# Relational graph layer on one core: h of pairs three to five transposed by DMA, in place of quarter products for S1 T1

## The chip, the cores and the metric

One core of a Trainium2 chip runs the whole program. The metric is the device time of one execution in microseconds. Every time below was measured on the chip, and the profile is one execution as the hardware profiler took it. Engine names are those of the profile: PE is TensorE, PEld its weight loads, DVE is VectorE, ACT is ScalarE, POOL is GpSimd and SP is SyncE, which here only issues DMAs.

## The reference, cut to what matters

```
h = maximum(layernorm(x), 0)                      # x is [1250, 1024], float32
out = h @ root + bias
for r in range(8):                                # 20000 edges (src, dst), each with a type
    sums = segment_sum(h[src] * (edge_type == r)[:, None], dst, n)
    cnt  = segment_sum(edge_type == r, dst, n)
    out += (sums / maximum(cnt, 1)[:, None]) @ weight[r]
u = out
z = concatenate([u, h], 1) @ w_gate + b_gate
y = x + tanh(u) * z + h * (1 - z)
```

## The kernel before

The 1250 rows are ten blocks of 128 (the last has 98), taken in five pairs: pair i is blocks i and i + 5, numbered from 0, so pairs "three to five" of the title are i = 2, 3, 4. Eleven matrices (eight weights, root, two halves of the gate) are multiplied one after another; s counts the matrices. For s < 10 the operand is h, and it stays in SBUF transposed, in `h_op[i]`, seven slots of 128 x 4 x 128 float32: A11, A12, A22 and the Winograd sums S1, S2, S3 (in A21's place) and S4.

`product` (line 445) does one pair with one matrix as seven products of quarters instead of eight. One of them, `add` at line 461, is four matmuls of 128 x 512, which the trace shows as eight records. After each product PE's result leaves PSUM by a copy on ACT or an addition on DVE, and `done()` (line 464) makes a "call": `between(j)` lets other work be written into the instruction streams at that place. The engines' queues are in order, so the place of a call decides what waits behind what.

From the second matrix on, some of the seven products of two neighbouring pairs are themselves split into seven products of half size. Such a one is two matmuls of 128 x 256 (line 227). `First` (line 329) does it for A11, `Second` (line 194) for A12, `Third` (from s = 4 on) for S4, and `Fifth` (line 372, s = 1 to 4, `FIFTHS`) for S1 times T1. `Fifth` forms sums on DVE twice (lines 281 to 290), copies half-banks on ACT (lines 396, 404 and 411), adds on DVE (lines 406 and 417), and uses a PSUM bank for each of its two results, `ps_n` and `ps_m`. The rest of PSUM is a ring of three banks `ps` (line 123), two banks `ps_b`, in which a pair's main sum grows, and `ps_q`.

While the first matrix is multiplied (s = 0) two generators fill the calls. `norms` (line 1319) makes h for the pairs: statistics on DVE, the scaled relu on ACT (line 965), two stores of 512 KB to `h_dram` on SP (line 970), `transposed` (line 419: eight PE transposes per block into `ps` banks, copied out by ACT at line 433 and DVE at line 431), x + h on DVE, stored at line 976, and `left` (line 437) for the four sums on DVE. `index` (line 1380) sorts the edges into a table. In groups of four chunks of edges it makes one-hot matrices on ACT (lines 1154, 1156, 1215, 1216), counts and looks up with small matmuls on PE (lines 1168 and 1223), picks and ranks on DVE (lines 1208 to 1258), loads keys through SP (line 1187), and after every fourth group writes 16 columns of the table by indirect DMAs on POOL (line 1262). `zip_longest` (line 1389) moves both on by one step at each call, and `on` (line 1395) leaves out five places of each later matrix. The index ends during s = 3. Its rows are used from s = 5 on, when POOL gathers rows of the products (line 1437) and DVE adds them up (line 1442) beside PE.

Of the kernel before, what the change touches and what calls it, by code (L numbers as in the profile page):

```python
# [12 lines left out]
I16 = mybir.dt.int16  # L13
AF = mybir.ActivationFunctionType
# [6 lines left out]
def tile_rgcn_highway(  # L21
# [61 lines left out]
    TICK = 9  # L83
    FIFTHS = 4
# [38 lines left out]
    def bank():  # L123
        return psum.tile([P, 512], F32, name="ps", bufs=3)

    def sum_bank(odd):

        return psum.tile([P, CG, P], F32, name=("ps_n", "ps_m")[odd], bufs=1).rearrange(
            "p c k -> p (c k)")
# [137 lines left out]
    class Third:  # L267
# [24 lines left out]
        def hold(self):  # L292
            self.c0 = sum_bank(0)
            return self.c0
# [77 lines left out]
    class Fifth:  # L372

        def __init__(self, f, i, room, p5):
            b = f.place["t1"]
            self.b11, self.b12, self.b21, self.b22 = [
                b[:, k:k + 2, c:c + H] for k in (0, 2) for c in (0, H)]  # L380
            self.a11, self.a12, self.a21, self.a22 = [
                h_op[i + o][:, S1, k:k + 2] for o in (0, 1) for k in (0, 2)]
            self.t1, self.t2, self.s1, self.s2 = room
            self.p5 = p5

        def sums(self):
            Third.sums(self)

        def next_sums(self):
            Third.next_sums(self)  # L390

        def begin(self):
            self.to0 = sum_bank(0)
            self.x = bank()[:, :H]
            Second.add(self, self.x, self.a11, self.b11, True)
            nc.scalar.copy(self.to0[:, :H], self.x)

        def second(self):
            Second.add(self, self.to0[:, :H], self.a12, self.b21)

        def early(self):
            y = bank()[:, :H]
            Second.add(self, y, self.s1, self.t1, True)
            nc.scalar.copy(self.p5, y)
            Second.add(self, self.x, self.s2, self.t2)
            nc.vector.tensor_add(self.to0[:, H:], self.x, self.p5)

        def late(self):
            self.to1 = sum_bank(1)
            Second.add(self, self.x, self.s1, self.t1)  # L410
            nc.scalar.copy(self.to1.rearrange("p (a n) -> p a n", a=2),
                           self.x[:, None, :].to_broadcast([P, 2, H]))
            Second.add(self, self.to0[:, H:], self.s2, self.b22)
            Second.add(self, self.to1[:, :H], self.a22, self.t2)

        def fifth_to(self):
            nc.vector.tensor_add(self.to1[:, H:], self.to1[:, H:], self.p5)

# [17 lines left out]

    def left(aop, parts=range(4)):

        for k in parts:
            to, add, a, b = ((S1, True, A21, A22), (S2, False, S1, A11), (S4, False, A12, S2),  # L440
                             (S3, False, A11, A21))[k]
            (nc.vector.tensor_add if add else nc.vector.tensor_sub)(aop[:, to], aop[:, a],
                                                                     aop[:, b])

    def product(aop, w, to, between=lambda j: None, last=None, pieces=1, whole=True,
                fill=None, second=None, third=None, inner=None, first=None, early=None, own=(),
                aside=None, head=False, lone=False, odd=0, root=None):
# [21 lines left out]
        def filled(name):  # L469
            if fill and name in fill and fill[name]():  # L470
                done()
                return True
            return False
# [10 lines left out]
        def p7():  # L484
# [3 lines left out]
            if root and head:  # L488
                between(TICK)
                root.late()  # L490
                nc.scalar.copy(c22, c)
                root.fifth_to()
# [20 lines left out]
        def p1():  # L513
# [5 lines left out]
            if root and head:  # L519
                root.sums()  # L520
                first.fifth_to()
            nc.scalar.copy(c11, b)
            if root and head:
                root.second()
# [4 lines left out]
        def p5(c=None):  # L529
            if root:  # L530
                c = root.to1
            elif c is None:
                c = inner.hold() if inner and inner.holds else sum_bank(odd)
# [9 lines left out]
        if root and head:  # L543
            root.begin()
            c = root.to0
            if inner:
                inner.c0 = c
            b = p1()
        elif first and head and early is None and "first" not in fill:
            c = inner.hold() if inner else sum_bank(odd)  # L550
# [15 lines left out]
        if root and head:  # L566
            root.early()
            root.next_sums()
        if not filled("sixth") and root and head:
            done()  # L570
# [67 lines left out]
    def fifths(s):  # L638

        return 0 < s <= FIFTHS  # L640

    waiting, waiting_third, waiting_first, waiting_fifth = {}, {}, {}, {}
# [10 lines left out]
    def step(s, i, between=lambda j: None, second=None):  # L653
# [8 lines left out]
        if two and i % 2 == 0:  # L662
            waiting[i] = Second(fac[s], i), t[0]
            if fifths(s):
                waiting_fifth[s, i] = Fifth(fac[s], i, room, p5_room)
# [13 lines left out]
        def beside(j):  # L679
# [6 lines left out]
            if two and i % 2 == 0 and j == 3:  # L686
                if not root:
                    waiting_first[s, i].fifth_to()
# [14 lines left out]
            if (s, i, j) == (0, 0, 3) or (s > 0 and (i, j) == (3, int(thirds(s) or fifths(s)))):  # L703
# [28 lines left out]
        root = waiting_fifth.get((s, i - i % 2)) if two else None  # L732
# [11 lines left out]
        if two:  # L744
# [30 lines left out]
            elif i == 2 and root and q:  # L775
                fill = dict(seventh=lambda: (e.first(), q.second(q.c0), True),
# [1132 lines left out]
```

## Time and profile before

| what | value |
|---|---|
| median of three executions | 1391.94 us |
| range of the three | 1385.30 to 1395.03 us |
| the profiled execution | 1385.30 us |
| its span, first to last instruction | 1383.5 us |
| busy in that span: PE, DVE, POOL, ACT | 1335.2, 992.4, 575.9, 381.3 us |
| mean granted clock of PE | 0.986 |

The profile gives, for each engine, the time in which at least one of its instructions ran. A matmul's end is modelled, and consecutive matmuls overlap, so what one costs in a stream is read from start to start and not from its duration. In a timeline line, the first two numbers are start and length in us, `x8` is the number of records merged, and the square bracket gives how long the engine had been idle and who ended the wait. "remote" there means that the profile names no releaser.

### The profile page before, as it was taken

The page shows a single profiled execution, that of the slowest core. Times are in us where ns is not written, and L with a number is a line of the kernel's source. Part 1 is how long each engine was busy: PE and PEld are TensorE (multiplying, and loading weights), DVE is VectorE, ACT ScalarE, POOL GpSimd, SP SyncE. Part 2 cuts the span into 40 slices and gives each one's busy share as a digit, 9 for nine tenths or more (in the row PEclk, how much of TensorE's full clock was granted, in tenths as well). Part 3 has the DMA queues.
Part 4 walks back from the last instruction along what each step waited for, and adds up shares of the span by engine and source line. Part 5 has one row for each costly group of instructions (what it writes and reads, how often), then busy time and mean ns, then how long its engine had stood idle before and what let it go on. Part 6 is the DMA issues. An engine that isn't in the chain of part 4 may idle for free.

```text
span 1383.5 us, 13746 instructions
## 1 busy us (share of the span) xinstructions
PE 1335.2 (97%) x4264; PEld 746.0 (54%) x4264; DVE 992.4 (72%) x1905; ACT 381.3 (28%) x818; POOL 575.9 (42%) x509
## 2 busy tenths in 40 slices
PE   9999987889989999999999999999999999999997
PEld 5444544445645554665565565566556556544443
DVE  7765844476637575655888898798688789857875
ACT  3465534536441221221111112122111111221210
POOL 0005544435355224620345346554545556624631
PEclk9999989899999999999999999999999999999999
DMA  9766322524154326114556878987968976888971
GB/s 321 275 196 111 78 66 39 180 84 67 56 141 94 86 72 128 45 63 141 193 179 216 272 242 281 341 267 239 330 223 294 331 261 202 279 307 252 337 191 58
DMA packets 104322, 260.61 MB, mean 188 GB/s; under 512 B 20670, under 2 KB 32338, under 8 KB 104112
## 3 DMA queue, kind: packets, MB, share of 16 engines
q0 software_dynamic: 44064, 118.20, 27.0%
q1 hardware_dynamic: 44048, 109.48, 24.7%
q10 hardware_dynamic: 16128, 31.98, 8.1%
q8 instruction: 34, 0.56, 0.2%
q14 instruction: 48, 0.39, 0.1%
HBM read 202.34 MB, written 75.41 MB: 201 GB/s over the span
## 4 chain that ended last, share of the span: by engine, by line
PE 79%; issue 7%; DVE 3%; ACT 3%; POOL 3%; DMA 2%; another core or an unknown queue 2%; POOLq 0%; SPq 0%; ACTq 0%; DVEq 0%
PE ps_b L461 39%; PE ps L227 13%; PE ps_m L461 9%; PE ps_n L461 5%; PE ps_b L227 3%; PE ps_n L227 2%; PE ps_q L227 2%; PE ps_q L461 2%; DMA got<-y,idx 2%; PE ps L461 2%; PE ps_m L227 1%; POOL got L1437 1%; PE ps L426 1%; ACT is_lo L1154 1%
## 5 line engine op out<-in xcount | busy, mean ns | idle before, releaser
L461 PE MATMUL ps_b<-w,h_op 128*128 128x512 f32 x1464 | 667.0, 600 | 7.6 <-ACT row L564 6.8
L461 PEld LDWEIGHTS ps_b<-w,h_op 128*128 128x128 f32 x1464 | 277.0, 192 | 318.0 <-issue 300.8
L1437 POOL DMA_INDIRECT got<-y,idx x193 | 248.2, 1286 | 288.5 <-DVE u L1442 184.9
L1442 DVE SCALAR_TENSOR_TENSOR u<-got,w_of,u 128x1024 f32<-128x1024 f32 (+1 forms) x193 | 246.9, 1282 | 33.1 <-DMA got<-y,idx 29.2
L1262 POOL DMA_INDIRECT table<-row_col,at_i x157 | 170.5, 1086 | 204.8 <-DVE at_i L1258 127.3
L461 PE MATMUL ps_m<-w,h_op 128*128 128x512 f32 x352 | 158.8, 594 | 1.1 <-DVE row L324 1.1
L461 PEld LDWEIGHTS ps_m<-w,h_op 128*128 128x128 f32 x352 | 66.3, 190 | 77.2 <-issue 72.9
L461 PE MATMUL ps_n<-w,h_op 128*128 128x512 f32 x208 | 94.6, 593 | 0.0
L227 PE MATMUL ps<-inner,inner 128*128 128x256 f32 x360 | 92.3, 383 | 0.0
L227 PE MATMUL ps<-w,h_op 128*128 128x256 f32 x320 | 84.4, 387 | 3.3 <-ACT w L244 3.3
L564 ACT COPY row<-ps_b 128x512 f32<-128x512 f32 x54 | 31.6, 585 | 201.0 <-PE ps_b L461 186.7
L487 ACT COPY row<-ps_b 128x512 f32<-128x512 f32 x53 | 31.0, 585 | 197.4 <-PE ps_b L461 194.8
L227 PEld LDWEIGHTS ps<-inner,inner 128*128 128x128 f32 x360 | 68.6, 192 | 18.6 <-issue 9.9
L227 PEld LDWEIGHTS ps<-w,h_op 128*128 128x128 f32 x320 | 60.2, 192 | 30.5 <-issue 20.1
L227 PE MATMUL ps<-w,w 128*128 128x256 f32 x288 | 73.9, 393 | 2.7 <-ACT w L233 2.7
L608 ACT COPY row<-ps_b 128x512 f32<-128x512 f32 x40 | 23.4, 584 | 179.2 <-PE ps_b L461 131.0
L227 PEld LDWEIGHTS ps<-w,w 128*128 128x128 f32 x288 | 56.4, 197 | 23.3 <-issue 13.4
L493 DVE TENSOR_TENSOR row<-row 128x512 f32<-128x512 f32 x44 | 30.2, 687 | 47.9 <-ACT row L487 42.9
L461 PEld LDWEIGHTS ps_n<-w,h_op 128*128 128x128 f32 x208 | 39.2, 190 | 44.1 <-issue 43.1
L1244 DVE SCALAR_TENSOR_TENSOR junk<-k_bc,key_col,before 128x128 f32<-128x128 int16 x157 | 55.0, 350 | 4.2
L1231 DVE TENSOR_TENSOR own<-ps_q,is_at 128x160 f32<-128x160 f32 (+1 forms) x40 | 12.7, 318 | 58.3 <-remote 37.3
L1154 ACT ACTIVATE is_lo<-io,less_lo 128x128 bf16<-128x128 f32 x157 | 50.1, 392 | 8.2 <-remote 5.3
(248 smaller groups left out, 1634.1 us busy)
## 6 DMA issues: line engine op xcount, KB each, us to landing
y<-row SPq DMA_DIRECT2D x72, 512.0 KB
w<-in_L_gnn_weight_dram ACTq DMA_DIRECT2D x21, 1024.0 KB
w<-in_L_gnn_weight_dram SPq DMA_DIRECT2D x10, 1024.0 KB
w<-in_L_gnn_w_gate_dram ACTq DMA_DIRECT2D x6, 1024.0 KB
k_bc<-keys_dram SPq DMA_DIRECT2D x39, 128.0 KB
l_bc<-los_dram SPq DMA_DIRECT2D x39, 128.0 KB
h_dram<-h_op SPq DMA_DIRECT2D x9, 512.0 KB
u<-in_L_gnn_bias_dram SPq DMA_DIRECT2D x9, 512.0 KB
```

The lines of the kernel that those rows point to most:

```text
L227: nc.tensor.matmul(p, a[:, k, :], b[:, k, :], start=(fresh and k == 0), stop=(k == 1), skip_group_check=True)
L426: nc.tensor.transpose(p[:, i, :n], of[:n, k * P:(k + 1) * P], ident[:n, :n])
L461: nc.tensor.matmul(b[:, at], aop[:, i, k, :], w.of[i][:, k, at], start=(fresh and k == 0), stop=(k == KQ - 1), skip_group_check=True)
L487: nc.scalar.copy(d, b)
L493: nc.vector.tensor_add(c22, c if lone else c22, d)
L564: nc.scalar.copy(c12, b)
L608: nc.scalar.copy(c21, b)
L1154: nc.scalar.activation(is_lo[:, i, :], io, AF.Abs, bias=less_lo[:, c0 + i:c0 + i + 1])
L1244: nc.vector.scalar_tensor_tensor(junk, o["k_bc"][:, i, :], key_col[:, c:c + 1], before, op0=OP.is_equal, op1=OP.mult, accum_out=rank[:, c: ...
L1262: ins = nc.gpsimd.indirect_dma_start(out=table[:, :], out_offset=bass.IndirectOffsetOnAxis(ap=at_i[:n, c:c + 1], axis=0), in_=row_col[:n, ...
L1437: nc.gpsimd.indirect_dma_start(out=t[:n], out_offset=None, in_=y[g][:, :], in_offset=bass.IndirectOffsetOnAxis(ap=at[:n, d, k:k + 1], axis=0),
L1442: nc.vector.scalar_tensor_tensor(u[:n], t[:n], w, u[:n], op0=OP.mult, op1=OP.add)
```

## The change

Two parts are exchanged. `Fifth` and all that calls it are taken out: in the matrices s = 1 to 4, S1 times T1 is again one whole product for each pair. Its banks go: `ps` becomes a ring of four, the sum c of S1, S4 is held in a bank of that ring (in `ps_n` only where `Third` holds it, and for the last matrix), and `ps_m` is gone.

In the first matrix, h of pairs i = 2, 3, 4 no longer goes through PE. For each block ACT splits the float32 numbers into a plane of low and a plane of high two-byte halves (`in_halves`), a DMA issued by SP transposes the 128 x 2048 two-byte numbers from SBUF to SBUF (`turned`), and ACT and DVE write the halves back into place, one quarter each (`whole_again`). The work buffers are free slots of `h_op`, and `room_all`, which is the four former `inner` tiles as one. The steps of `norms` are put in a new order around this.

The two generators are joined anew: at calls that are marked HEAVY the index is not moved on. Four calls are marked, and one empty step more is in `columns`. In the later matrices `on` leaves out three places in place of five. Counted in the code, the first count step of the index comes one call later than before, from the fourth pair on each step comes four calls later, and the last step comes with matrix s = 4, first pair, call 2, where it came with s = 3, last pair, call 6.

```
-    FIFTHS = 4
...
-        return psum.tile([P, 512], F32, name="ps", bufs=3)
-
-    def sum_bank(odd):
-
-        return psum.tile([P, CG, P], F32, name=("ps_n", "ps_m")[odd], bufs=1).rearrange(
-            "p c k -> p (c k)")
+        return psum.tile([P, 512], F32, name="ps", bufs=4)
...
-    class Fifth:
...
+    def in_halves(of, n, to):
+
+        if n < P:
+            nc.gpsimd.memset(to[n // 32 * 32:], 0.0)
+        nc.scalar.copy(to.bitcast(U16)[:n].rearrange("p (h c) -> p h c", h=2),
+                       of.bitcast(U16)[:n].rearrange("p (c h) -> p h c", h=2))
+
+    def turned(of, to):
+
+        nc.sync.dma_start_transpose(to.bitcast(U16).rearrange("p (c r) -> p c r", r=P),
+                                    of.bitcast(U16))
+
+    def whole_again(aop, part, of, n):
+
+        of = of.bitcast(U16).rearrange("p (h a k r) -> p h a k r", h=2, a=2, r=P)
+        for a, to in enumerate(((A11, A12), (A21, A22))[part]):
+            (nc.vector.tensor_copy if a else nc.scalar.copy)(
+                aop[:, to].bitcast(U16).rearrange("p k (r h) -> p h k r", h=2)[..., :n],
+                of[:, :, a, :, :n])
+            if n < P:
+                nc.gpsimd.memset(aop[:, to, :, n:], 0.0)
...
         def p5(c=None):
-            if root:
-                c = root.to1
-            elif c is None:
-                c = inner.hold() if inner and inner.holds else sum_bank(odd)
+            if c is None:
+                c = inner.hold() if inner and inner.holds else held("ps_n")
                 add(c, S1, True)
...
-        if root and head:
-            root.begin()
-            c = root.to0
-            if inner:
-                inner.c0 = c
-            b = p1()
-        elif first and head and early is None and "first" not in fill:
-            c = inner.hold() if inner else sum_bank(odd)
+        if first and head and early is None and "first" not in fill:
+            c = inner.hold() if inner else bank()
             add(c, S1, True, ks=range(KQ // 2))
             b = p1()
             p5(c)
...
+        def turn(i, blocks, second, *of):
...
+            to, of = (room_all[:, :D], flat(second)), [flat(t) for t in of]
+            for part in range(2):
+                b = blocks[part]
+                in_halves(b.ht, b.n, of[part])
+                turned(of[part], to[part])
+                yield
+            for part in range(2):
+                whole_again(h_op[i], part, to[part], blocks[part].n)
+                yield
...
             both(*b2)
-            yield
+            for b in b1:
+                b.with_x()
+            yield
+            turn_of = turn(2, b2, h_op[3][:, 0:2], h_op[3][:, S2:S3 + 1], h_op[4][:, S2:S3 + 1])
+            next(turn_of)
             for b in b2:
                 b.store()
             yield
-            for b in b1:
-                b.with_x()
-            yield
-            factored(2, b2)
+            next(turn_of)
+            yield
             b2[0].with_x(b2[0].ht)
             b2[1].with_x()
+            x4 = [load_x(4, 0)]
+            yield
+            next(turn_of)
+            yield
+            next(turn_of)
+            yield
             left(h_op[2])
...
-        todo = (None for _ in zip_longest(norms(), index()))
+        def norms_and_index():
+
+            later = index()
+            for heavy in norms():
+                if not heavy:
+                    next(later)
+                yield
+            yield from later
+
+        todo = norms_and_index()
...
-                if s > 0 and (i, j) in ((0, 0), (1, 1), (1, 5), (3, 1), (NP - 1, 4)):
+                if s > 0 and (i, j) in ((0, 0), (1, 5), (NP - 1, 4)):
                     return
```

The lines of the diff that are not shown do the same for pairs i = 3 and 4, take the arguments and calls of `Fifth` out of `product`, `beside` and `step`, and add the type `U16`.

## The prediction

> **What bounds the kernel now.** I read the page's shares first, then the stretches, then TensorE's timeline, then who it waits for. Over the span PE is busy 1335.2 of 1383.5 us, so a step on PE's own list counts in full and one elsewhere only where PE waits for it. The page's mean hides three stages, which the stretches show (columns: us, then busy time and instructions of PE, PEld, DVE, ACT, POOL, then granted clock, DMA share, GB/s):
>
> ```profile
> core 0: us, PE busy (x) PEld busy (x) DVE busy (x) ACT busy (x) POOL busy (x), PEclk, DMA share, GB/s
> 50.00:100.00 50.00, 49.65 (x182) 24.97 (x181) 36.90 (x97) 31.78 (x69) 0.20 (x1) 1.00 0.64 228
> 200.00:250.00 50.00, 37.51 (x150) 23.17 (x149) 21.29 (x84) 22.45 (x57) 15.65 (x16) 0.88 0.20 37
> 400.00:500.00 100.00, 100.00 (x330) 57.62 (x330) 65.12 (x155) 23.46 (x51) 33.77 (x29) 1.00 0.41 105
> ```
>
> The first matrix (to about 126 us) fills PE; ACT has a third of the stretch free, DVE a quarter. The later matrices fill PE wholly. Between lies the index phase: PE idles and its clock falls. TensorE's timeline shows the places that the diff touches:
>
> ```profile
> 49.87 1.95 PE L426 MATMUL ps<-ident,h_op 128*128 128x128 f32 x16
> 51.65 3.60 PE L461 MATMUL ps_b<-w,h_op 128*128 128x512 f32 x8
> ...
> 65.39 1.47 PE L426 MATMUL ps<-ident,h_op 128*128 128x128 f32 x12
> 67.21 0.65 PE L426 MATMUL ps<-ident,h_op 128*128 128x128 f32 x4 [0.35 <-DVE h_op L431]
> 81.84 1.04 PE L426 MATMUL ps<-ident,h_op 128*128 128x128 f32 x8
> 93.62 0.84 PE L426 MATMUL ps<-ident,xt 98*128 98x98 f32 x8
> ```
> ```profile
> 159.56 1.03 PE L227 MATMUL ps<-inner,inner 128*128 128x256 f32 x4
> 160.42 1.03 PE L227 MATMUL ps_n<-w,inner 128*128 128x256 f32 x4
> 162.86 1.13 PE L227 MATMUL ps_m<-inner,h_op 128*128 128x256 f32 x4 [1.41 <-ACT ps_m L411]
> ...
> 247.01 0.39 PE L1223 MATMUL ps_q<-s_b,to_lo 128*128 128x40 bf16 x4 [10.17 <-DVE s_b L1208]
> 282.99 6.51 PE L461 MATMUL ps_b<-w,h_op 128*128 128x512 f32 x8 [4.68 <-ACT row L564]
> ```
>
> A row starts with start and duration; the bracket is the idle time before it and who ended it. Ends are modelled, so I take spacing from the next start: 51.65−49.87 = 1.78 us for 16 transposes; 160.42−159.56 = 0.86 for a quarter product (4 records); 3.43 for a whole product of 8.
>
> **The change part by part.**
>
> *Transposes off PE.* Pairs 2, 3 and 4 had the L426 rows at 49.87 (1.78 us), 65.39 to 67.70 (2.31 with its wait of 0.35), 81.84 (0.87 of spacing) and 93.62 (0.68): −5.6 us.
>
> *Seven quarters become two wholes.* `Fifth` gives 7 × 0.86 = 6.01 us for the S1·T1 of two pairs; two whole products take 2 × 3.43 = 6.87. That is +0.86 for each couple, two couples in each of the matrices 1 to 4: 8 × 0.86 = +6.9 us. DVE and ACT lose its sums (about 5.3 and 1.3 us a couple); in this stretch they are half idle, so I give nothing for that here, and a rival below prices it.
>
> *Fifth's own wait.* The row at 162.86 waits 1.41 us for ACT to empty ps_m. The trace has this wait four times (1.41, 1.41, 0.41, 0.41), and it goes with the products: −3.6 us. Late next is the ring, which follows.
>
> *Four ring banks in place of three and ps_m.* For matrices 1, 2 and 3, the first half of S1 of the first pair now takes the ring bank that the last pair's S4 has just filled, and so waits for the addition that empties it. In before that is the row on VectorE's timeline:
>
> ```profile
> 145.24 0.69 DVE L480 TENSOR_TENSOR row<-row,ps_m 128x512 f32<-128x512 f32 x1 [2.17 <-PE ps_m L461]
> ```
>
> S4's product ends at 145.20, the addition at 145.93: about 0.85 us with the hand-over, three times, +2.5 us. Queued behind it on PE is everything, as PE works in order. The upper end is that row falling behind a burst (rival 3).
>
> *ACT's splitting in the first matrix.* Each of six blocks gets a copy of 2048 two-byte elements and part of the joining; the evictions of L433 go. Nearest rows:
>
> ```profile
> 42.42 1.24 ACT L965 ACTIVATE h_op<-h_op,less,rs 128x1024 f32<-128x1024 f32 x1 [0.52 <-DVE less L949]
> ...
> 45.42 0.56 ACT L538 COPY row<-ps_m 128x512 f32<-128x512 f32 x1
> 50.51 0.60 ACT L433 ACTIVATE h_op<-ps 128x512 f32<-128x512 f32 x1 [4.04 <-PE ps L426]
> ```
>
> By the row of 1.24 for 1024 elements a split takes 2.5 us and a joined quarter 1.24, against an eviction of 0.60: 6 × (2.5 + 1.24 − 0.60) = +19 us on ACT between 42 and 112 us. ACT has some 18 free in each 50. What is queued behind a split are the copies of product banks (row 45.42), and PE waits for those only when one is late by more than a product of 3.43 us. I take +1 us. Ends: 0 if the splits fall between copies; 15 if each of six makes PE wait a whole split. DVE's joining adds some 3 us in a stretch with 13 free: nothing, and were that cover gone, 3 us.
>
> *The six transposing DMAs.* Each moves 512 KB from SBUF to SBUF on SP's queue; no row of before shows one. Call its time d. Low end: at the 415 GB/s that plain transfers reach in this stage, 1.3 us. High end: 2048 pieces of 256 bytes, each as costly as a mean packet of queue q1 (24.7% × 16 × 1383.5 / 44048 = 0.124 us), over 16 engines: 15.9 us. Small packets in this trace cost far less: q0 from 126 to 400 us has 3845 in 1.1% of 16 × 274 us, 12.5 ns each; twice that for the 256 bytes gives 24 ns and d = 3.1. I take 3, nearest to the small packets since the bytes are contiguous. SP's queue around them:
>
> ```profile
> 44.40 1.47 SPq L970 DMA_DIRECT2D h_dram<-h_op  x2
> 46.40 7.62 SPq L976 DMA_DIRECT2D xh_dram<-h_op  x3
> ```
>
> The xh stores of pair 1 (46.40) are issued ahead of them, the 1 MB of pair 2's h stores between the two. The first transpose can start near 48.5 (45.4 + 0.6 + 2.5); pair 2's S1 comes at 63.6 by now (67.82 less the transposes gone). With 2 us for joining and summing, nothing waits while d ≤ 3.8; pair 3 has room to 6.7, pair 4 to 5.6. The stall is 2(d−3.8) + 2(d−6.7) + (d−5.6), each term from its threshold: 0 at d = 3, 14 at d = 8, 53 at 15.9. I take 0.
>
> [...]
>
> *The index.* Counted in the code, its steps end four calls later than in before (about 10.5 us at 2.6 us a call), whatever the change says. Its readers have room: the index loads (POOL L836) end at 595.4 and the first DVE reader (L873) starts at 616.9, 21 us. Cost 0 while that cover lasts; were it gone, 10.5. The bursts of 16 indirect DMAs move with the steps and meet other products, priced below.
>
> *Sum:* −5.6 + 6.9 − 3.6 + 2.5 + 1 = +1.2 us. On the profiled execution (1385.3 us, span 1383.5) that is 1386.5. This execution is the lowest of the three, 6.6 below their median; on the median's scale it is 1391.9 + 1.2 = 1393.
>
> **The rivals.**
>
> *1. Transposes land late (slower).* For it: 2048 pieces each, on queues that already move up to 426 GB/s, behind stores. Against: room of 3.8 to 6.7 us. It decides at d = 8 (+14); at d = 9 the stall is 18.4, so 1393 + 18 = 1411.
>
> *2. The index phase heals (faster).* Between 126 and 420 us PE idles 34.5 us and spends 37.4 at half clock, some 14 us lost; nearly all lies in the table bursts of POOL L1262, where DVE and ACT get PE's results late:
>
> ```profile
> 246.40 0.33 DVE L1231 TENSOR_TENSOR own<-ps_q,is_at 128x160 f32<-128x160 f32 x1 [13.37 <-remote]
> ```
>
> For it: `Fifth` chains small products through DVE and ACT, and with it go 42 us of DVE and 10 of ACT, so PE meets fewer hand-overs in a burst. Against: the ten bursts stay, and 282.99 waits for a copy (L564) that stays too. It decides when over a quarter of the 48.5 us goes; a third is −16: 1393 − 16 = 1377.
>
> *3. The ring wait falls into the bursts (slower).* The new wait of 0.85 us needs DVE just after S4. In a burst a hand-over took 10.17 us (row 247.01). Three at 10 in place of 0.85 are +27 less some cover: 1393 + 25 = 1418. Against: a burst holds about 20 us in every eight calls, and S4 of the last pair at 145 fell outside. Two of three must be hit to pass 1%.
>
> *4. The index move does nothing.* Probably true, and inside the forecast.
>
> **How the numbers follow.** One per cent, about what a measurement here can tell from no change, is 14 us: faster is below 1378, slower above 1406. The forecast's case (costs as taken, bursts as costly as before) has 0.55, from 1384 to 1404 on its own: the 6.6 us between executions below, ACT's 10 above. Rival 1 gets 0.16, rival 2 0.15, rival 3 0.14. Faster 0.15 is rival 2; slower 0.30 is rivals 1 and 3; within 0.55. The range takes in rival 2's third and rival 3 with 3 us of scatter: 1377 to 1421; outside are d above 9.5 and a healing beyond a third.
>
> **What would show it.** No L426-like transposes on PE for pairs 2 to 4. The landing time of the transposing DMAs against 3 us, and whether PE's first products of pairs 2 to 4 name a joining step as releaser: if not, rival 1 falls. PE's idle time in 126 to 420 against 34.5 us, and its half-clock time against 37.4, decide rival 2. S1's first half after S4 three times with about 0.85 us of wait on DVE's addition; 5 or more is rival 3. S1 of whole products: 3.43 spacing. The prediction is wrong if PE waits in 40 to 126 us for more than 5 us in all, if the index phase moves by over 14 us either way, or if a wait stands before the first gather near 616 us.

## The result, and the profile after

| | time, us | against the kernel before |
|---|---|---|
| before, 20 runs | 1388.66 (1384.12 to 1396.63) | |
| after, 20 runs | 1381.85 (1374.99 to 1385.04) | ratio 0.9943, 95% interval 0.993 to 0.9957 |
| after once more, beside 13 runs of before (1390.92) | 1380.7 | ratio 0.9913, 0.9881 to 0.9945 |

The change made the kernel 0.6% faster, some 7 us, where 1 us slower was forecast. That is inside the 1% band and inside the range, but the sign is not the one that the sum gave, and the interval excludes it. The sum was near by luck: two of its terms, one wrong by 23 to 27 us and one by 16 to 22, cancel.

The two profiled executions (1385.30 and 1383.35 us) lie nearer to each other than the medians do. A second pair of profiles, taken in the experiments, is 5.6 us apart (spans 1385.2 and 1379.6), so I use both pairs. Three marks on TensorE's timeline divide an execution. They are the first half-size product of matrices 1, 2 and 3 (counted from 0), which has the same place in every version:

| us | matrix 1 begins | matrices 1 and 2 take | matrix 3 to the end of the span |
|---|---|---|---|
| before, two profiles | 133.90, 134.24 | 292.2, 291.7 | 957.4, 959.3 |
| after, two profiles | 128.17, 128.09 | 294.3, 293.0 | 959.1, 958.5 |

So the first matrix gains 5.7 to 6.2 us. The two matrices beside which the index runs lose 1 to 2 us, though whole products should cost them +3.4. What follows changes by less than two profiles of one kernel differ. Matrices 1 and 2 as one stretch, with the columns of the stretches shown before, first before, then after:

```profile
133.90:426.14 292.24, 257.74 (x951) 145.82 (x948) 167.48 (x609) 136.83 (x336) 135.36 (x127) 0.94 0.38 90
```
```profile
128.17:422.47 294.30, 262.00 (x913) 136.63 (x912) 152.75 (x587) 139.31 (x342) 139.19 (x131) 0.93 0.38 91
```

In both PE stands still for over 30 us and the granted clock is 0.93 to 0.94. Who ends the waits has changed. TensorE's timeline of after, the rows with a wait:

```profile
46.14 3.70 PE L430 MATMUL ps<-w,h_op 128*128 128x512 f32 x8 [0.35 <-ACT row L493]
...
175.93 1.13 PE L221 MATMUL ps<-w,w 128*128 128x256 f32 x4 [1.86 <-issue]
179.55 6.26 PE L430 MATMUL ps_b<-w,h_op 128*128 128x512 f32 x8 [2.49 <-ACT row L513]
210.89 0.26 PE L1154 MATMUL ps_q<-s_b,to_lo 128*128 128x40 bf16 x4 [3.77 <-issue]
216.20 6.71 PE L430 MATMUL ps_b<-w,h_op 128*128 128x512 f32 x8 [2.23 <-ACT row L513]
261.67 0.29 PE L1154 MATMUL ps_q<-s_b,to_lo 128*128 128x40 bf16 x4 [5.46 <-DVE s_b L1139]
...
328.94 6.65 PE L430 MATMUL ps_b<-w,h_op 128*128 128x512 f32 x8 [3.45 <-ACT row L513]
362.08 0.25 PE L1154 MATMUL ps_q<-s_b,to_lo 128*128 128x40 bf16 x4 [5.17 <-DVE s_b L1139]
410.16 5.31 PE L430 MATMUL ps_b<-w,h_op 128*128 128x512 f32 x8 [3.39 <-ACT row L481]
```

The 16 and 12 transposes on PE and the wait of 1.41 us for ps_m (row 162.86 of before) are gone. Every wait after 160 us stands in a run of sixteen table DMAs on POOL or ends at most 5.4 us behind it. With two more, they come to 32 us. In before such waits (4.11, 10.17, 4.68 and 1.93) come to 21, and others are mixed in. The row after a long wait is often stretched as well: the product at 179.55 takes 6.26 us, where one at full clock takes 3.60; from 178 to 184.5 us the granted clock is 0.50.

The new DMAs on SP's timeline, and two rows of ACT's:

```profile
48.61 3.72 SPq L393 DMA_TRANSPOSE inner<-h_op  x1
52.40 1.03 SPq L900 DMA_DIRECT2D h_dram<-h_op  x2
53.53 4.21 SPq L393 DMA_TRANSPOSE h_op<-h_op  x1
```
```profile
46.69 1.90 ACT L388 COPY h_op<-h_op 128x2048 uint16<-128x2048 uint16 x1 [0.60 <-ACT row L493]
...
59.50 1.34 ACT L400 COPY h_op<-h_op 128x1024 uint16<-128x1024 uint16 x1 [3.46 <-DMA h_op<-h_op]
```

The second transpose of the pair is issued from 53.53 on, and ACT, which waits for it, starts at 59.50. By their semaphores all six land 4.3 to 6.0 us after the start of the issue. SP needs 2.0 to 4.2 us to issue one, against 0.5 for a plain store of the same size (the row of two at 52.40; the 80 stores of L616, 72 of them of that size, have a median of 0.32 and at most 1.19, while a load of x at the start takes 2.52). Still PE waits only 0.35 us in the whole stretch from 40 to 126 us.

### The profile page after: what moved, and what is told of

Its sections match the earlier page's. It is cut to its first block, busy times and chain, and to the rows that moved or that the text cites. A ratio compares the mean times of both kernels' runs of the same rounds, so it can differ in the third digit from the quotient of the medians.

```text
span 1381.6 us, 13340 instructions
## 1 busy us (share of the span) xinstructions
PE 1337.4 (97%) x4120; PEld 723.2 (52%) x4120; DVE 957.3 (69%) x1825; ACT 386.7 (28%) x800; POOL 581.3 (42%) x510
## 4 chain that ended last, share of the span: by engine, by line
PE 83%; issue 4%; DMA 3%; another core or an unknown queue 3%; ACT 2%; DVE 2%; POOL 1%; SPq 1%; POOLq 0%; DVEq 0%
PE ps_b L430 40%; PE ps L430 16%; PE ps L221 13%; PE ps_n L430 4%; PE ps_b L221 3%; PE ps_q L221 2%; PE ps_q L430 2%; PE ps_n L221 1%; DMA xt<-in_x_dram 1%; DMA got<-hr_dram,node 1%; DMA w<-in_L_gnn_weight_dram 1%; ACT is_lo L1085 1%; POOL out_dram L770 1%; DMA k_bc<-keys_dram 1%
## 5 line engine op out<-in xcount | busy, mean ns | idle before, releaser
L1415 POOL DMA_INDIRECT got<-y,idx x193 | 251.1, 1301 | 286.9 <-DVE u L1420 179.1
L430 PE MATMUL ps<-w,h_op 128*128 128x512 f32 (+1 forms) x592 | 267.2, 593 | 0.3 <-ACT row L493 0.3
L430 PEld LDWEIGHTS ps<-w,h_op 128*128 128x128 f32 x592 | 112.0, 192 | 122.6 <-issue 117.1
L454 ACT COPY row<-ps_b 128x512 f32<-128x512 f32 x53 | 31.1, 586 | 194.5 <-PE ps_b L430 178.8
L430 PE MATMUL ps_n<-w,h_op 128*128 128x512 f32 x176 | 80.1, 592 | 0.0
L513 ACT COPY row<-ps_b 128x512 f32<-128x512 f32 x54 | 31.6, 586 | 163.1 <-PE ps_b L430 154.3
L221 PE MATMUL ps<-w,h_op 128*128 128x256 f32 x288 | 75.4, 385 | 0.0
L553 ACT COPY row<-ps_b 128x512 f32<-128x512 f32 x40 | 23.4, 585 | 170.1 <-PE ps_b L430 117.7
L221 PEld LDWEIGHTS ps<-w,h_op 128*128 128x128 f32 x288 | 54.6, 192 | 27.7 <-issue 22.1
L221 PE MATMUL ps<-inner 128*128 128x256 f32 x264 | 67.8, 379 | 0.0
L221 PEld LDWEIGHTS ps<-inner 128*128 128x128 f32 x264 | 50.1, 190 | 14.9 <-issue 8.4
L430 PEld LDWEIGHTS ps_n<-w,h_op 128*128 128x128 f32 x176 | 33.4, 190 | 39.5 <-issue 39.0
L481 ACT COPY row<-ps_b 128x512 f32<-128x512 f32 x54 | 31.7, 586 | 79.4 <-PE ps_b L430 67.0
```

Source lines behind the costliest of these rows:

```text
L221: nc.tensor.matmul(p, a[:, k, :], b[:, k, :], start=(fresh and k == 0), stop=(k == 1), skip_group_check=True)
L430: nc.tensor.matmul(b[:, at], aop[:, i, k, :], w.of[i][:, k, at], start=(fresh and k == 0), stop=(k == KQ - 1), skip_group_check=True)
L454: nc.scalar.copy(d, b)
L513: nc.scalar.copy(c12, b)
L553: nc.scalar.copy(c21, b)
L1415: nc.gpsimd.indirect_dma_start(out=t[:n], out_offset=None, in_=y[g][:, :], in_offset=bass.IndirectOffsetOnAxis(ap=at[:n, d, k:k + 1], axis=0),
```

## The experiments

All are named by what they differ in. Each group ran on a chip of its own, beside its own runs of the kernel before. In the third group that kernel took 1356 us and not 1389 to 1392, and this difference turned out to be part of the answer. The last column is from the one profiled execution of each kernel. For e1 and e3 that was the fastest of its kernel (5.6 and 6.9 us below the median), for e4 and e8 the slowest (4.8 and 4.7 above), so these four stretches are good to some 5 to 7 us.

| kernel | us | ratio to before, 95% interval | matrices 1 and 2, us |
|---|---|---|---|
| group 1: before | 1388.65 | | |
| e0_before_again | 1388.15 | 1.000, 0.9982 to 1.0018 | 291.7 |
| e1_no_fifth | 1364.98 | 0.985, 0.9821 to 0.9878 | 262.8 |
| e2_index_four_sooner | 1411.82 | 1.0178, 1.015 to 1.0207 | 298.2 |
| e3_transposes_on_pe | 1386.30 | 0.9985, 0.9967 to 1.0004 | 283.7 |
| group 2: before | 1391.73 | | |
| e4_no_fifth_index_later | 1388.97 | 0.9967, 0.9948 to 0.9987 | 294.5 |
| e5_no_fifth_fours | 1342.78 | 0.9649, 0.9603 to 0.9695 | 244.4 |
| e6_after_fours | 1345.28 | 0.9662, 0.9617 to 0.9708 | 252.4 |
| e7_after_twos | 1380.96 | 0.9925, 0.9903 to 0.9947 | 295.7 |
| group 3: before | 1356.26 | | |
| e8_after_fours_sooner | 1348.44 | 0.9947, 0.993 to 0.9963 | 249.3 |
| e9_after_eights | 1342.77 | 0.9904, 0.9887 to 0.992 | 244.7 |
| e10_before_fours | 1356.61 | 1.0005, 0.9989 to 1.0021 | 264.2 |
| e11_sooner_padding_on_dve | 1336.30 | 0.9858, 0.9842 to 0.9875 | 244.4 |
| group 4: before | 1390.92 | | |
| e12_after_again | 1380.70 | 0.9913, 0.9881 to 0.9945 | 293.0 |
| e13_no_fifth_again | 1370.51 | 0.9833, 0.98 to 0.9866 | 269.7 |
| e14_padding_on_dve_again | 1390.32 | 0.9983, 0.9954 to 1.0011 | 290.8 |
| e15_eights_again | 1373.15 | 0.9856, 0.9824 to 0.9887 | 276.5 |
| group 5: before | 1392.11 | | |
| e16_fours_padding_on_dve | 1341.07 | 0.9643, 0.9597 to 0.969 | 252.1 |
| e17_no_fifth_fours_again | 1342.90 | 0.9649, 0.9607 to 0.9691 | 244.3 |

### The change taken apart (group 1)

The control, the kernel before unchanged:

> The kernel before, once more, for a second profile of it and as a control of the comparison: ratio 1.000, within 0.002. If the index phase (126 to 420 us) varies from execution to execution, its loss on PE (time beyond the full-speed spacing of its products, 55.5 us in the first profile) comes out several us different here, and the longest waits stand at other places of the bursts; if it is fixed, the loss is 55 to 56 again.

The loss was the same, with the longest waits at the same runs (10.2 us near 247 and 4.1 near 198 again). Three others changed in size: 4.68 became 1.15, 1.19 became 2.89 and 1.30 became 3.17 us.

`Fifth` left out alone:

```
-    FIFTHS = 4
+    FIFTHS = 0
```

> The kernel before with S1 T1 of two pairs as two whole products in all matrices, nothing else of the change: transposes on TensorE, the index where it was (give or take a call). Theory A (products and their own waits only): 8 x 0.83 = +6.6 us of products, -3.6 of Fifth's waits, so +3 us, ratio 1.002. Rival B (the small dependent products also lengthen the table bursts, and that goes with them): 5 to 6 us less than A, ratio 0.998 or lower, and the index phase loses 45 to 50 us on PE in place of 52 to 55.

Measured: 24 us faster, far below what either theory allowed. The stretch of matrices 1 and 2 shows where:

```profile
134.18:397.00 262.82, 248.86 (x900) 132.13 (x896) 147.35 (x556) 132.51 (x323) 131.18 (x121) 0.98 0.49 100
```

It is 29 us shorter than in before, although it holds 3.4 us more of products. (This execution is 5.6 us below its median.)

The index moved on at every call, in the kernel after:

```
-        HEAVY = True
+        HEAVY = False
```

> The kernel after with the index moved on at every call, so that from the fourth pair on its steps come four calls sooner, as in the kernel before. Theory C (what the change gave beyond the transposes comes from where the table bursts fall among the products): 4 to 6 us slower than the kernel after, near 1387 us, ratio 0.998 to 1.000. Rival (placement does nothing in the mean): like the kernel after, 1382 us, ratio 0.994 to 0.996.

Both were wrong: 30 us slower than after. One wait makes 20 of them. TensorE's timeline, then POOL's, then VectorE's:

```profile
137.64 5.25 PE L430 MATMUL ps<-w,h_op 128*128 128x512 f32 x8 [20.07 <-issue]
...
191.34 0.25 PE L1154 MATMUL ps_q<-s_b,to_lo 128*128 128x40 bf16 x4 [4.60 <-DVE s_b L1139]
...
298.04 5.27 PE L430 MATMUL ps_b<-w,h_op 128*128 128x512 f32 x8 [4.62 <-ACT row L513]
```
```profile
115.79 1.16 POOL L1193 DMA_INDIRECT table<-row_col,at_i  x1 [14.61 <-DVE at_i L1189]
...
135.50 0.98 POOL L1193 DMA_INDIRECT table<-row_col,at_i  x1 [0.31 <-issue]
136.52 0.34 POOL L404 MEMSET h_op<- 128x120 f32 x2
```
```profile
136.89 2.74 DVE L411 TENSOR_TENSOR h_op<-h_op 128x512 f32<-128x512 f32 x4 [20.16 <-POOL h_op L404]
```

Two settings to zero of 0.2 us each (L404, the padding of the 98-row block) are queued on POOL behind sixteen indirect DMAs. DVE's sums wait for them, and PE for the sums. In after the same settings come before the first run, which the four HEAVY calls see to. The seven other waits of over 4 us in this kernel have one thing in common: PE goes on 2.4 to 2.9 us after the last table DMA of a run ended on POOL (at 188.9 and 295.2 us for the two shown).

The transposes of pairs 2 to 4 back on PE, in the kernel after:

```
-                in_halves(b.ht, b.n, of[part])
-                turned(of[part], to[part])
+                transposed(h_op[i], part, b.ht, b.n)
                 yield
...
-                whole_again(h_op[i], part, to[part], blocks[part].n)
```

> The kernel after with the transposes of pairs 2 to 4 back on TensorE, in the calls where the halves are split now; no splitting, no transposing DMAs, no joining. If the DMA transposes give what the removed products took: +5.7 us on the kernel after, 1387.5 us, ratio 0.999, all of it before 130 us. If they also cost something that no wait on PE shows (contention of the stores and weight loads behind them): less than +4, ratio under 0.998. If the index phase profits from the free DMA queues in another way, the difference is above 7.

Measured 1386.3, 4.4 above after. Matrix 1 begins at 134.38 in place of 128.17, so the 6.2 us before it are the transposes.

The three steps follow one another: before to e1_no_fifth 0.985, on to e3 0.9985, on to after 0.9943. Leaving `Fifth` out gives 24 us, something in the later index takes 19 back, and the transposes give 4 to 6.

### Where the index falls, and the runs of sixteen (group 2)

e1_no_fifth with four more empty steps in `columns`, so that all later index steps come four calls later:

```
             yield
             yield
+            yield
+            yield
+            yield
+            yield
```

> The kernel before without the seven quarter products (as e1_no_fifth, 1365 us), and every index step after the columns four calls later. Theory C (where the table bursts fall among the products decides, and four calls later is a bad place): the bursts cost PE 45 to 55 us in place of 24, 1385 to 1395 us. Rival D (the four ring banks, or the other places left out, made the kernel after slower than e1_no_fifth, not the four calls): 1365 us again, within 4.

Measured 1389.0, matrices 1 and 2 in 294.5 us. The four calls alone cost 16 us, most of what e3 had lost, so it is the place of the index and not the ring. PE's waits in matrices 1 and 2 grow with them from 14.0 us (e1) to 33.6.

Next, the table's indirect DMAs in groups of four, in e1_no_fifth and in after:

```
-    AT = 4
+    AT = 1
```

> As e1_no_fifth (1365 us), with the table's indirect DMAs issued four at a time, each group of four when its ranks are known, in place of sixteen at a time. Theory E (it is the unbroken run of sixteen that holds up the signals from PE): the index phase's loss falls from 24 to under 10 us, 1350 us. Rival F (each indirect DMA costs its share wherever it stands): 24 again, 1365 us; four DVE operations more per group stay off PE's path.

> As the kernel after (1382 us), with the table's indirect DMAs issued four at a time. Theory E: the loss of 55 us in the index phase falls under 15, 1342 us, and the kernel comes out 4 to 6 us ahead of e5_no_fifth_fours, which is what the transposes by DMA give. Rival F: 1382 us, within 5.

Both fell by more than 20 us. e6, expected 4 to 6 us ahead of e5, is 2.5 behind it: in matrices 1 and 2 the later place of the index still costs 8 us (252.4 against 244.4). Group 5 shows why. In e5 PE hardly waits in matrices 1 and 2:

```profile
138.36:382.74 244.38, 243.89 (x900) 130.21 (x897) 157.74 (x640) 132.95 (x323) 132.26 (x122) 1.00 0.53 107
```

The last of the group wrote the sixteen DMAs into the stream two at a call:

```
-                for c in range(c0, c1):
+                due.extend(range(c0, c1))
...
                     if f is None:
+                        scatter(2)
                         yield
```

> As the kernel after, with the same sixteen indirect DMAs made known together but issued two at a call over eight calls. Theory E: as e6_after_fours or 2 to 5 us better, near 1340 us; the waits on PE that end with a burst are gone. Rival F: 1382 us, within 5; then PE's waits are spread over the calls but sum up to 50 us.

Measured as after, but this tells nothing of theory E. POOL's timeline shows the same unbroken run:

```profile
155.96 1.18 POOL L1196 DMA_INDIRECT table<-row_col,at_i  x1 [8.04 <-DVE at_i L1189]
...
175.94 0.98 POOL L1196 DMA_INDIRECT table<-row_col,at_i  x1 [0.30 <-issue]
```

All sixteen wait for the same `at_i` and nothing else, and POOL takes one every 1.3 us, though they stand two at a call in the code. Groups of four are spaced because each needs ranks of its own.

### A chip without the hold-up, and the two causes apart (groups 3 and 4)

e8 has both edits, `AT = 1` and `HEAVY = False`, in the kernel after:

> The kernel after with the table's DMAs four at a time and the index moved on at every call (four calls sooner from the fourth pair on). Theory E (only long runs of these DMAs hurt; once they are gone the index's place is free): within 4 us of e6_after_fours, 1341 to 1349 us, where the same four calls cost 30 us with runs of sixteen. Rival: the place matters for another reason, and it is 10 us or more slower.

e9, the kernel after with groups of eight:

```
-    AT = 4
+    AT = 2
```

> The kernel after with the table's DMAs eight at a time, a dose between sixteen (55 us lost on PE between 100 and 450 us, 1382 us) and four (18 us, 1345 us). Theory E, a run holds a signal up until it ends: runs of 10 us, and part of them covered by work that PE already has: 25 to 40 us lost, 1352 to 1367 us. Rival (a threshold, such as more than eight of these DMAs in flight): as with four, 1345 us, within 3.

e10 is the kernel before with `AT = 1`:

> The kernel before, with its seven quarter products, and the table's DMAs four at a time. Theory E: what leaving the quarter products out saved (24 us) came from the runs of sixteen, so here they are worth what they were designed for: -6.6 of products, +3.6 of own waits against e5_no_fifth_fours, 1340 us, between 1336 and 1343. Rival B (the quarter products themselves cost the index phase, whatever the runs): 1355 to 1365 us.

e11 is e2 with one line more, in `whole_again`:

```
             if n < P:
-                nc.gpsimd.memset(aop[:, to, :, n:], 0.0)
+                nc.vector.memset(aop[:, to, :, n:], 0.0)
```

> As e2_index_four_sooner (1412 us), with the padding of the joined blocks set to zero on DVE in place of POOL. There the two settings stood behind sixteen table DMAs on POOL, and PE waited 20.2 us for the sums behind them. If that is the cause: 1412 - 20 = 1392 us, between 1386 and 1396, still above the kernel after by what the other runs of sixteen cost at that place. If PE's wait there is the same signal hold-up as elsewhere: 1407 us or more.

The kernel before took 1356 us on this chip, and fours left it there (1356.6), so times from this group do not compare with those of group 2. e8 and e9 tell little of theory E here; what they lose is mostly one wait each (6.58 and 7.29 us) for padding behind the table DMAs. e10 landed where rival B had put it. e11, with all its runs of sixteen, has no wait over 0.5 us in matrices 1 and 2. I therefore ran four kernels again, with what each would show on either kind of chip. The chip of group 4 was of the first kind:

> The kernel after, unchanged, beside the kernel before on one chip. In the last group of runs the kernel before took 1356 us where it had taken 1389 to 1392 on other chips, and no wait on PE ended with a run of sixteen table DMAs. Theory E with G (the signals are held up during those runs on some chips only; the quarter products' own waits are there on every chip): if before takes about 1356 here, after takes 1334 to 1342, some 18 us less; if before takes about 1390, after takes 1380 to 1384 again. Rival H (the gain is 7 us on every chip): near 1349 in the first case.

> The kernel before without the quarter products, unchanged from e1_no_fifth. Theory G (the quarter products bring waits of their own on PE and the clock's fall behind them, near 20 us net of their saving, wherever the runs of sixteen fall): 18 to 24 us less than before on this chip too, whichever its level. Rival (their removal only moved other work out of the runs of sixteen): with before at 1356, no gain or +3 us.

> The kernel after with the index sooner and the padding set to zero on DVE, unchanged from e11. With before at about 1390 (signals held up): 1412 less the 20 us behind POOL, 1388 to 1396. With before at about 1356: 1336 again.

> The kernel after with the table's DMAs eight at a time, unchanged from e9. With before at about 1390: theory E, between four at a time (1345) and sixteen (1382), 1352 to 1367 us; a threshold above eight: 1345. With before at about 1356: 1343 again, most of its loss being the one wait near 121 us.

e12, e13 and e14 came in as the theories with a hold-up said. e14 and e11 are one kernel on two chips, 1390 and 1336 us. A hand-over in a run of sixteen, in e14: VectorE's row, then the last DMA of the run on POOL, then TensorE's.

```profile
233.22 0.33 DVE L1162 TENSOR_TENSOR own<-ps_q,is_at 128x160 f32<-128x160 f32 x1 [10.76 <-remote]
```
```profile
229.75 0.98 POOL L1193 DMA_INDIRECT table<-row_col,at_i  x1 [0.31 <-issue]
```
```profile
223.20 0.26 PE L1154 MATMUL ps_q<-s_b,to_lo 128*128 128x40 bf16 x4
...
233.83 0.39 PE L1154 MATMUL ps_q<-s_b,to_lo 128*128 128x40 bf16 x4 [6.74 <-DVE s_b L1139]
```

PE made ps_q at 223.20, and DVE, idle since 222.46, reads it at 233.22, 2.5 us after the run ended (229.75 + 0.98). PE, which needs what DVE makes of it, waits 6.74 us. In e11, in the middle of a run (230.3 to 252.1), the same step on VectorE:

```profile
240.17 0.33 DVE L1162 TENSOR_TENSOR own<-ps_q,is_at 128x160 f32<-128x160 f32 x1 [4.25 <-PE ps_q L1099]
```

There PE's two groups of small products began at 239.77 and 239.88, so the hand-over took 0.3 us. So on the chips of groups 1, 2 and 4 PE's signals to DVE and ACT come late, by up to some 10 us, while a run of these DMAs goes on, and on that of group 3 they do not.

e15 missed its range (1373 against 1352 to 1367), and its rows say why. The first of TensorE's waits of over 2 us:

```profile
184.41 1.13 PE L221 MATMUL ps<-w,w 128*128 128x256 f32 x4 [2.67 <-issue]
189.02 5.98 PE L430 MATMUL ps_b<-w,h_op 128*128 128x512 f32 x8 [3.47 <-ACT row L513]
260.47 0.29 PE L1154 MATMUL ps_q<-s_b,to_lo 128*128 128x40 bf16 x4 [5.40 <-DVE s_b L1139]
```

By POOL's timeline two groups of eight stood together four times in this stretch, three times without a gap and once with one of 1.7 us (165.3 to 186.6 and 237.0 to 257.4 are the first two), and all waits of over 2 us lie in or just behind these four. The single eights, 10 us long (199.6 to 209.7, 219.8 to 229.8), have none. In e5 sixteen DMAs in fours, with gaps, take 24 us and cause no wait.

The second cause is seen in e10, on the chip without the hold-up. Its stretch of matrices 1 and 2, with the quarter products:

```profile
134.45:398.67 264.22, 249.28 (x952) 142.25 (x948) 179.34 (x697) 136.56 (x336) 135.00 (x126) 0.97 0.52 99
```

The whole products need 244.3 to 244.7 here, on either kind of chip (e5, e9, e11, e17), so the quarters should need 3.4 less, 241. They need 23 us more than that. Nearly two thirds of it stand as waits on TensorE's timeline:

```profile
163.34 1.13 PE L227 MATMUL ps_m<-inner,h_op 128*128 128x256 f32 x4 [1.42 <-ACT ps_m L411]
176.32 2.78 PE L227 MATMUL ps<-w,w 128*128 128x256 f32 x8 [2.65 <-ACT w L233]
...
233.83 3.70 PE L461 MATMUL ps_b<-w,h_op 128*128 128x512 f32 x8 [1.34 <-ACT row L522]
...
307.26 3.58 PE L227 MATMUL ps<-w,w 128*128 128x256 f32 x8 [2.65 <-ACT w L233]
```

With seven more, these come to 14.5 us; the granted clock of 0.97 in the row above, over 264 us, is another 8 or so. What stood before the second of them on ACT:

```profile
173.91 1.27 ACT L1154 ACTIVATE is_lo<-io,less_lo 128x128 bf16<-128x128 f32 x4
175.22 0.63 ACT L1156 ACTIVATE is_lo<-is_lo 128x512 bf16<-128x512 bf16 x1
175.75 0.24 ACT L1201 CAST s_b<-seen 128x80 bf16<-128x80 f32 x1
175.90 0.36 ACT L233 COPY w<-ps 128x256 f32<-128x256 f32 x1
```

PE had the half bank ready near 173.5, but ACT first made a group of one-hots of the index (2.2 us). The copy at L233 is not `Fifth`'s: it belongs to `Second`, which every kernel here has. Where `Fifth` is left out, the whole product of S1 stands on PE before the one that needs the half bank again. The same place in e17, TensorE and then ScalarE:

```profile
171.51 3.60 PE L461 MATMUL ps_m<-w,h_op 128*128 128x512 f32 x8
174.94 1.89 PE L227 MATMUL ps<-w,w 128*128 128x256 f32 x8
```
```profile
173.91 0.36 ACT L233 COPY w<-ps 128x256 f32<-128x256 f32 x1
```

ACT makes the same one-hots first, but PE is busy meanwhile and waits for nothing. So this wait comes from what the quarter products take away, the work that covered a hand-over.

### A version that beats both (group 5)

The kernel after with table DMAs in fours and both paddings on DVE, beside e5 once more:

> The kernel after with the table's DMAs four at a time and both paddings of the short block set to zero on DVE, so that neither stands behind those DMAs on POOL. Where before takes about 1390: e6_after_fours took 1345 with some 5 us of waits at 110 to 117 us behind POOL; without these 1338 to 1342. Where before takes about 1356: 1334 to 1338. Rival: the waits at 117 us were not POOL's, and it takes 1345 again.

> The kernel before without the quarter products and with the table's DMAs four at a time, unchanged from e5. Beside e16 on one chip it tells what the transposes by DMA are worth once the index phase is quiet: by the rows removed, e16 should be 5 to 6 us ahead (1343 against 1338). Where before takes about 1390: 1343 again. Where it takes about 1356: 1338 to 1344, since this kernel has hardly any hold-up left.

e16 took 1341.1 us, 3.6% less than before, and e17 1342.9. The gap is 2 us, not 5 to 6, and the intervals overlap. Matrix 1 begins 8.2 us earlier in e16 (128.51 against 136.75; e17 itself begins it some 2.7 us later than before does, with a wait of 2.12 us behind a run of twelve table DMAs), but its matrices 1 and 2 take 252.1 against 244.3. Some waits are left there, on TensorE's timeline:

```profile
175.01 2.08 PE L221 MATMUL ps<-w,w 128*128 128x256 f32 x4 [2.37 <-ACT w L233]
300.89 1.13 PE L221 MATMUL ps<-w,w 128*128 128x256 f32 x4 [0.97 <-ACT w L233]
```

The traces show what makes them. In e16 groups of four follow one another without a pause, as unbroken runs of twelve. The first and the last DMA of such a run on POOL, a product on TensorE, and the copy of its result on ScalarE:

```profile
156.27 1.19 POOL L1193 DMA_INDIRECT table<-row_col,at_i  x1 [1.48 <-DVE at_i L1189]
...
171.42 0.98 POOL L1193 DMA_INDIRECT table<-row_col,at_i  x1 [0.30 <-issue]
```
```profile
163.58 3.60 PE L430 MATMUL ps<-w,h_op 128*128 128x512 f32 x8
```
```profile
172.12 0.59 ACT L493 COPY row<-ps 128x512 f32<-128x512 f32 x1 [5.49 <-remote]
```

The product is done near 167, and ACT takes it up 5 us later. The one-hots and the copy of w queue behind that, and PE waits at 175.01. In e9, on the chip of group 3 and inside a run of sixteen, the same copy:

```profile
177.50 0.58 ACT L493 COPY row<-ps 128x512 f32<-128x512 f32 x1 [0.60 <-PE ps L430]
```

e16's other waits in this stretch, from 1.02 to 0.63 us, lie in or at most 3 us behind such runs of twelve too, and e6 has the same; in e5 and e17 no run in this stretch is longer than eight. So what is left in e16 is the hold-up again, and with it the chip of group 5 is the fourth that shows it. Which of e16's differences from e17 makes the groups run together was not tried.

## Why the prediction was wrong

*Right, with its size.* "Transposes off PE" at −5.6: matrix 1 begins 5.7 to 6.2 us earlier. "Seven quarters become two wholes" at +6.9, half of it in matrices 1 and 2: the start-to-start spacings of which it is made are unchanged, but no run shows the sum by itself. ACT's splitting, taken at +1, costs nothing: a split takes 1.90 where 2.5 was taken, and PE's one wait of 0.35 (at 46.14) ended before the first split began (46.69).

*"Fifth's own wait", −3.6, and "I give nothing for that here".* This is the first step that failed. I counted the four waits that named ps_m and put the other waits down to the table bursts. Two rows for ACT's copies of w were in the profile of before:

```profile
175.85 3.63 PE L227 MATMUL ps<-w,w 128*128 128x256 f32 x8 [2.65 <-ACT w L233]
...
386.62 1.13 PE L227 MATMUL ps<-w,h_op 128*128 128x256 f32 x4 [2.80 <-ACT w L244]
```

Both come back in e10 on the chip without the hold-up (2.65 and 1.86), so no burst is needed for them. Half idle on the mean, ACT still stood with index work in front of a copy that PE, without the whole product between, needed at once. On that chip this is 23 us in matrices 1 and 2, where I had 3.6 in all. Measured alone on the chips of groups 1 and 4, leaving `Fifth` out gives −24 and −20 us in place of +3.

*"The index. Cost 0".* This is the second. I asked only whether its readers would wait, and they do not. But the runs of sixteen that it moves hold up PE's signals, and four calls later they meet, as I read it, products that need them sooner: 0.985 becomes 0.9967 by the four calls alone (e4; in another group) and 0.9985 with all of it (e3), 16 to 19 us. The prediction said that the bursts "meet other products, priced below", and then took them "as costly as before".

*"Four ring banks", +2.5.* No wait stands at that place in after: 0.

*The transposing DMAs.* They land 4.3 to 6.0 us after their issue starts, not 3; 2.0 to 4.2 us of that SP spends on the issue. That is over the room of 3.8 us worked out for pair 2, and yet PE waits for none of them, so the room was under-reckoned. Rival 1 falls. The issue was four to eight times as long as that of the plain stores at 52.40 (0.5 us each). The landing was no later than a plain one's: by the same semaphores, the plain loads of x and stores that SP issued between 41 and 113 us landed 2.6 to 6.5 us after their issue started.

*The rivals.* Rival 2 had the right place but saw one cause where there are two. The quarter products' chain heals by nearly all of its own waits, on each of the chips where that was tried, while, if the two causes add, what the bursts cost grows from about 28 us (292.2 less the 264.2 of e10) to about 50 (294.3 less 244.4). Rival 3, a wait for a ring bank in a burst, is not seen. Rival 4, that the index move does nothing, called probably true, is refuted by e4. For matrices 1 and 2 this makes −23 + 3.4 + 22 = +2; it has to agree with their profiles, since each term is a difference of the same stretches, and so it proves nothing more. With −5.7 for the first matrix and +1.7 behind matrix 3 that is the −1.9 of the profiled pair. The medians are some 5 us further apart than that pair; the second pair (5.6 us) is near them, and I can't name the place of the rest.

*Two slips in the sums.* The formula for the stall gives 13.4 us at d = 8, where +14 stands, and the upper end of the range, 28 us above 1393, is reached at d = 10.9 and not at 9.5. Neither decided anything.

*Open.* Why the signals come late, and why not on one chip. That groups of four cure it where at most eight DMAs follow one another, and groups of eight only where two don't touch, speaks for the length of an unbroken run; twelve were enough for a late signal in e16. A limit on how many of these DMAs are under way would give the same, and no run tells them apart.

## What to carry to other kernels

When every wait of a stretch is put down to one suspect, take the releasers row by row: an engine that is half idle can still have a two-microsecond job in front of the copy that the bound engine needs (in e10, 2.2 us of one-hots on ACT, and 2.65 us of wait on PE). When a step moves, price what its neighbours will meet, not only whether its reader waits. A long unbroken run on one queue can hold up a small thing that stands behind it (in e2, two settings of 0.2 us behind sixteen DMAs, and 20.07 us of wait on PE), and DMAs that waited for one value were not spaced by spreading them in the code (e7, sixteen in 21 us); give each small group its own value to wait for, and look on the queue's timeline whether the groups really stand apart (in e5 they did, in e16 they ran together by twelve).

## What was not expected of the hardware

- While sixteen indirect DMAs ran on POOL without a gap (some 20 us), DVE and ACT took up PE's results up to some 10 us late, on three of five chips; a fourth, where no run of sixteen was profiled, showed 5 us in a run of twelve (16 us). In e2 seven of PE's waits ended 2.4 to 2.9 us after the run; in other kernels some ended inside it. Runs of eight (10 us, e15), and sixteen spread over 24 us with gaps (e5), showed none of it.
- One chip showed none at all: the same kernel took 1336 us there (e11) and 1390 on another (e14).
- In after, issuing one transposing DMA of 512 KB held SP for 2.0 to 4.2 us, a plain store of that size beside them 0.5 (row 52.40).
- After many waits of over 2 us PE's clock is granted at half for a while (0.50 in after from 178 to 184.5, 212.5 to 222 and 325 to 334.5 us): products of 3.60 us took 5.3 to 6.7 (rows 179.55, 216.20, 328.94, 410.16 of after), 1.7 to 3.1 us more each, on top of the waits of 2.2 to 3.5 us just before them. Not after all: behind waits of 2.49 us in e8 (at 129.06) and 2.12 us in e17 (at 125.82) the product took 3.70.
